# A two-layer graph attention kernel: projections as seven block products, sums through PSUM, two graphs in small steps, spread rows read with a stride

## The chip, the cores and the metric

The kernel runs on one core of a Trainium2 chip. A core has five engines that work side by side, each through its own queue in order: TensorE (PE in the profile; matrix products and transposes, into PSUM), VectorE (DVE), ScalarE (ACT), GpSimd (POOL) and SyncE (SP, which here only issues DMAs). The 128 partitions of the on-chip memory SBUF are the rows of every tile. PSUM has eight banks; one bank holds 512 f32 values per partition. An engine that needs what another makes waits on a semaphore, and so does one that wants to overwrite a buffer that another still reads.

The metric is the time of one execution on the device in microseconds (us). Before the change it is 3888.38 us, the median of three runs (3888.18 to 3889.19).

## The reference

There are 64 graphs of N = 256 nodes with 512 features each, and a 0/1 matrix `adj` of 256 x 256 per graph. Two layers are applied, both with a layer norm ahead and the input added behind. The first layer holds two graph attentions (4 heads of 256, then 1 head of 512), the second one (8 heads of 64). Cut to what matters:

```python
h = maximum(layernorm(x), 0)                      # layer 0
#   gat_layer, once with H=4, F=256 and once with H=1, F=512:
xl = (h @ W).reshape(B, N, H, F)
asrc, adst = einsum('bnhf,hf->bnh', xl, a_src), einsum('bnhf,hf->bnh', xl, a_dst)
e = leaky_relu(asrc[:, :, None, :] + adst[:, None, :, :], 0.2)
attn = softmax(where(mask[..., None], e, -1e9), axis=1)      # over the sources
out = einsum('bsdh,bshf->bdhf', attn, xl) + bias
#   between the two: elu
x = x + out
h = maximum(layernorm(x), 0)                      # layer 1
xp = h @ W_proj                                   # 8 heads of 64
scores = leaky_relu(a_src[:, :, :, None] + a_dst[:, :, None, :] + b_att, 0.2)
att = softmax(where(adj > 0, scores, -1e30), axis=-1)
x = x + relu(att @ xh)
```

So each graph needs three projections: 256 x 512 by 512 x 1024, 256 x 1024 by 1024 x 512, and 256 x 512 by 512 x 512, all in f32.

## The kernel before, in words

A graph's 256 nodes lie as two tiles of 128 (T = 2). `short_path` computes everything without subtracting a maximum in the softmax; at the end it checks that no exponential came too near the limits, and `general_path`, which is not run on this data, would do the work again.

The softmax weight of an edge is exp(leaky_relu(a + b)). The kernel writes it as a product of one-dimensional exponentials: for a source with value a and a target with value b, exp(0.2(a + b)) times the larger of 1 and exp(0.8(a + b)). It therefore needs only exponentials of per-node numbers, some of them spread over all partitions as rows, and one multiply and maximum per edge and head. The extra columns of the weight matrices (N1, N2, N3) make a projection give those per-node numbers (`ex1`, `ex2`, `ex3`) along with the features.

`steps(b)` is a generator with the work of one graph in eight pieces:

- piece 0: load x and adj (SP), build the mask (`mask`, `cap`; DVE, transposes on PE), layer norm, transposed and with relu (`norm_relu_t`, L106 to L128; its `rstd` is a power on GpSimd, L116), and x plus the second bias on GpSimd (L170);
- piece 1: first projection (L184: four blocks of columns, two node tiles, four chunks of 128 features each, so 32 products); ACT takes each result out of PSUM, scaled (L188);
- piece 2: edge weights `e` on DVE (L196), attention products (L204), division and bias (L207, L209), elu (L211 to L213);
- piece 3: transposes of z (L222) with copies on ACT or DVE (L223), second projection (L232: 32 products);
- piece 4: edge weights and products of the second attention (L243, L251), the sum with x (L257), layer norm again;
- piece 5: third projection (L268: 16 products), the exponentials (L271, L272);
- pieces 6 and 7: the eight heads in two groups of four: a weighing on ACT (`wy`, L286), the edge weight on DVE (L287), products with 65 columns (L294), division (L298), the last sum on GpSimd (L303), the store.

The per-node numbers reach all partitions through `over_partitions` (L131): two transposes of a few columns on PE (L135), a copy to SBUF (L137), a DMA of the rows to DRAM (L139) and a DMA that reads them back into every partition (L141). The rows lie whole, one head after the other.

Two graphs are in flight: `order` (L370) interleaves the eight pieces of a graph with those of the one before it. Within this, a scheduling layer places each engine's instructions when the kernel is built, by buffers that come free. Products use five PSUM banks (`ps_mm`), transposes three (`ps_tr`). Before the first graph the attention vectors are folded into the extra columns of the weights (GpSimd products, DVE sums; L337 to L363).

Of the kernel before, what the change touches and what calls it, by code (L numbers as in the profile page):

```python
# [8 lines left out]
F32 = mybir.dt.float32  # L9
BF16 = mybir.dt.bfloat16  # L10
I32 = mybir.dt.int32
# [26 lines left out]
def fold(nc, pool, name, dst, w, a, heads, width):  # L38

    prod = pool.tile([P, heads * width], F32, name=name)  # L40
    pv = prod.rearrange("p (h f) -> p h f", h=heads)
    nc.gpsimd.tensor_tensor(pv, w.rearrange("p (h f) -> p h f", h=heads), a, ALU.mult)
    nc.vector.tensor_reduce(dst, pv, AX.X, ALU.add)
# [3 lines left out]
def short_path(ctx, tc, flags, x, adj, w1, att_src1, att_dst1, b1, w2, att_src2, att_dst2, b2, w_proj, w_att,  # L47
# [13 lines left out]
    assert N == 2 * P and D == D2 == H3 * K3 == 512 and H1 == G and H3 == 2 * G and F1 == D2 // 2  # L61

    const = ctx.enter_context(tc.tile_pool(name="const", bufs=1))
    io = ctx.enter_context(tc.tile_pool(name="io", bufs=3))
# [3 lines left out]
    ps_mm = ctx.enter_context(tc.tile_pool(name="ps_mm", bufs=5, space=PSUM))  # L68
# [21 lines left out]
    N1, N2, N3 = 3 * H1, 3, 3 * H3  # L90
    w1_sb = const.tile([P, DC, HF + N1], F32, name="w1_sb")
    w2_sb = const.tile([P, HC, D2 + N2], F32, name="w2_sb")
    wp_sb = const.tile([P, DC, D + N3], F32, name="wp_sb")
    HALF = D2 // 2
# [3 lines left out]
    wb = const.tile([P, H3], F32, name="wb")  # L98
    xl3s = []
    for i in range(2):  # L100
        xl3 = const.tile([P, T, H3, K3 + 1], F32, name=f"xl3_{i}")
        nc.gpsimd.memset(xl3[:, :, :, K3:], 1.0)
        xl3s.append(xl3)


    def norm_relu_t(src):  # L106
# [14 lines left out]
        hT = work.tile([P, DC, N], F32, name="hT")  # L121
        for c2 in range(DC // 2):
            pt = ps_tr.tile([P, 2, N], F32, name="pt")
            for k in range(2):
                for t in range(T):
                    c = 2 * c2 + k
                    nc.tensor.transpose(pt[:, k, t * P:(t + 1) * P], h[:, t, c * P:(c + 1) * P], ident)  # L127
            nc.scalar.activation(hT[:, 2 * c2:2 * c2 + 2, :], pt, AF.Relu)  # L128
        return hT

    def over_partitions(w, n, bufs):  # L131

        pr = ps_tr.tile([P, 2, N], F32, name="pt")
        for t in range(T):
            nc.tensor.transpose(pr[:n, 0, t * P:(t + 1) * P], w[:, t, :], ident)  # L135
        row = small.tile([n, N], F32, name=f"row{n}", bufs=2)
        nc.vector.tensor_copy(row, pr[:n, 0, :])  # L137
        kept = dram.tile([n, N], F32, name=f"kept{n}")
        nc.sync.dma_start(kept, row)  # L139
        bc = work.tile([P, n, N], F32, name=f"bc{n}", bufs=bufs)  # L140
        nc.sync.dma_start(bc.rearrange("p h n -> p (h n)"), rows_of(kept, n * N))  # L141
        return bc


    def steps(b):
        xs = io.tile([P, T, D], F32, name="xs")
        nc.sync.dma_start(xs, x[b].rearrange("(t p) d -> p t d", p=P))
        ad = io.tile([P, T, N], I32, name="ad", bufs=2)
        nc.sync.dma_start(ad, adj[b].rearrange("(t p) n -> p t n", p=P))


        mask = work.tile([P, T, N], BF16, name="mask")
        nc.vector.scalar_tensor_tensor(mask, ad, 0.0, eye, ALU.is_gt, ALU.max)
        a01 = work.tile([P, T, N], BF16, name="a01")
        nc.vector.tensor_scalar(a01, ad, 0.0, None, ALU.is_gt)
        deg = small.tile([P, T], F32, name="deg")
        nc.vector.tensor_reduce(deg, a01, AX.X, ALU.add)
        none = small.tile([P, T], F32, name="none")
        nc.vector.tensor_scalar(none, deg, 0.5, EVEN, ALU.is_lt, ALU.mult)
        for t in range(T):  # L160
            nc.vector.tensor_scalar(a01[:, t, :], a01[:, t, :], OPEN, none[:, t:t + 1], ALU.mult, ALU.add)
        cap = work.tile([P, T, N], BF16, name="cap", bufs=3)
        pt = ps_tr.tile([P, T, N], BF16, name="pt")
        for t in range(T):
            for s in range(T):
                nc.tensor.transpose(pt[:, t, s * P:(s + 1) * P], a01[:, s, t * P:(t + 1) * P], ident_h)
        nc.any.tensor_copy(cap, pt)

        hT = norm_relu_t(xs)
        nc.gpsimd.tensor_tensor(xs, xs, b2_sb[:, None, :].to_broadcast([P, T, D]), ALU.add)  # L170
        exs = small.tile([P, T * (N1 + N2 + N3)], F32, name="exs")
        ex1 = exs[:, :T * N1].rearrange("p (t n) -> p t n", t=T)
        ex2 = exs[:, T * N1:T * (N1 + N2)].rearrange("p (t n) -> p t n", t=T)
        ex3 = exs[:, T * (N1 + N2):].rearrange("p (t n) -> p t n", t=T)
        yield

        xl = work.tile([P, T, H1, F1 + 1], F32, name="xl1", bufs=1)
        for k in range(H1):
            n = F1 + (N1 if k == 0 else 0)
            at = k * F1 + (N1 if k else 0)  # L180
            for t in range(T):
                pm = ps_mm.tile([P, 512], F32, name="pm")
                for c in range(DC):
                    nc.tensor.matmul(pm[:, :n], hT[:, c, t * P:(t + 1) * P], w1_sb[:, c, at:at + n],  # L184
                                     start=(c == 0), stop=(c == DC - 1))
                if k == 0:
                    nc.scalar.activation(ex1[:, t, :], pm[:, F1:n], AF.Exp)
                nc.scalar.activation(xl[:, t, k, :F1], pm[:, :F1], AF.Copy, scale=ex1[:, t, k:k + 1])  # L188
            if k == 0:
                bc1 = over_partitions(ex1[:, :, 2 * H1:], H1, 1)  # L190
                nc.gpsimd.tensor_copy(xl[:, :, :, F1], ex1[:, :, :H1])
        yield
        e = work.tile([P, T, H1, N], F32, name="e1", bufs=1)
        for h in range(H1):
            for s in range(T):
                nc.vector.scalar_tensor_tensor(e[:, s, h, :], bc1[:, h, :], ex1[:, s, H1 + h:H1 + h + 1],  # L196
                                               mask[:, s, :], ALU.max, ALU.mult)
        z = work.tile([P, T, HF], F32, name="z", bufs=1)
        ez = work.tile([P, T, HF], F32, name="ez", bufs=1)
        for t in range(T):  # L200
            for h in range(H1):
                pm = ps_mm.tile([P, 512], F32, name="pm")
                for s in range(T):
                    nc.tensor.matmul(pm[:, :F1 + 1], e[:, s, h, t * P:(t + 1) * P], xl[:, s, h, :],  # L204
                                     start=(s == 0), stop=(s == T - 1))
                r = small.tile([P, 1], F32, name="r1")
                nc.vector.reciprocal(r, pm[:, F1:F1 + 1])  # L207
                sl = slice(h * F1, (h + 1) * F1)
                nc.vector.scalar_tensor_tensor(z[:, t, sl], pm[:, :F1], r, b1_sb[:, sl], ALU.mult, ALU.add)  # L209

# [443 lines left out]
```

## Time and profile before

| | |
|---|---|
| median of three runs | 3888.38 us |
| the profiled execution | 3889.76 us |
| its span, first to last instruction | 3888.1 us |
| granted TensorE clock, mean | 0.989 |
| busy TensorE, DVE, ACT, GpSimd | 3701.8, 2244.3, 1289.7, 482.6 us |
| first product of the second graph | at 145.12 us |
| first product of the last graph | at 3787.07 us |
| one graph (1202.27 to 1260.99), busy TensorE | 58.72 us, 57.39 us |

How to read what follows. A row of a group names the line in the kernel, the engine, the operation, what it writes and reads, the shape and the count; behind the bars stand the busy time, the mean of one instruction in ns, the idle time of the engine ahead of it and what ended that. A row in order of time has the start, the length, the engine and the same names; in brackets the idle time ahead and what released it. Matmuls overlap one another, so the mean of one (380 ns) is longer than the distance between two starts. An f32 product of a 128 x 128 block shows as two records. Until 145 us the kernel is filling: weights are folded and only one graph runs.

### The profile page before, as it was taken

The numbers are of one execution on the slowest core, as the hardware profiler recorded it, in microseconds if no ns is written. First come the engines' busy times: TensorE is split into PE (matmuls) and PEld (weight loads), VectorE is DVE, ScalarE is ACT, GpSimd is POOL, SyncE is SP. The second block draws the span as 40 slices with busy tenths as digits, with TensorE's granted clock in tenths as the row PEclk, the third lists the DMA queues.
The fourth block names the chain that finished last, engine by engine and source line by source line (L and its number), as shares of the span: only waits on it lengthen the run. The fifth ranks groups of instructions, "written<-read, shape, count | busy, mean of one in ns | idle before, by whom it ended". The sixth has DMA issues, their size and how long they took to land. (4 is left out here: it accounts for less than half of the span.)

```text
span 3888.1 us, 51838 instructions
## 1 busy us (share of the span) xinstructions
PE 3701.8 (95%) x20100; PEld 3213.4 (83%) x20100; DVE 2244.3 (58%) x5780; ACT 1289.7 (33%) x3010; POOL 482.6 (12%) x448
## 2 busy tenths in 40 slices
PE   3799999999999999999999999999999999999998
PEld 2688888888888888888888888888888888888887
DVE  4555655655656556556556556556556556556554
ACT  0223323333333333333333333333333233233332
POOL 5111111111111111101101101101101111111110
PEclk8899999999999999999999999999999999999998
DMA  3011111111111111111111111111111111111111
GB/s 116 28 51 57 49 52 52 54 52 49 57 52 47 59 49 50 59 47 52 54 52 52 48 58 52 49 58 50 51 58 50 51 57 49 52 52 54 50 36 46
DMA packets 86828, 205.34 MB, mean 53 GB/s; under 512 B 7216, under 2 KB 36208, under 8 KB 78384
## 3 DMA queue, kind: packets, MB, share of 16 engines
q1 hardware_dynamic: 81536, 193.82, 14.5%
q10 hardware_dynamic: 4192, 5.24, 0.4%
q8 instruction: 162, 2.65, 0.3%
q0 software_dynamic: 848, 2.89, 0.2%
q14 instruction: 90, 0.74, 0.1%
HBM read 167.51 MB, written 34.41 MB: 52 GB/s over the span
## 5 line engine op out<-in xcount | busy, mean ns | idle before, releaser
L184 PE MATMUL pm<-w_sb,hT 128*128 128x256 f32 (+1 forms) x4096 | 927.9, 384 | 21.9 <-DVE w_sb L331 11.5
L232 PE MATMUL pm<-w_sb,h1T 128*128 128x259 f32 (+1 forms) x4096 | 915.0, 380 | 0.0
L184 PEld LDWEIGHTS pm<-w_sb,hT 128*128 128x128 f32 x4096 | 765.8, 191 | 141.1 <-DVE w_sb L331 13.1
L232 PEld LDWEIGHTS pm<-w_sb,h1T 128*128 128x128 f32 x4096 | 759.3, 189 | 122.2
L287 DVE SCALAR_TENSOR_TENSOR e<-wy,exs,cap 128x256 f32<-128x256 f32 x1024 | 433.3, 482 | 206.4 <-ACT wy L286 206.4
L204 PE MATMUL pm<-xl,e 128*128 128x257 f32 x2048 | 484.4, 384 | 29.4 <-DVE z L209 21.9
L268 PE MATMUL pm<-wp_sb,hT 128*128 128x280 f32 (+1 forms) x2048 | 491.5, 390 | 0.0
L286 ACT ACTIVATE wy<-bc,exs 128x256 f32<-128x256 f32 x1024 | 438.0, 501 | 159.5 <-DMA bc<-kept 155.7
L294 PEld LDWEIGHTS pm<-xl,e 128*128 128x128 f32 x4096 | 478.7, 194 | 7.5 <-DVE e L287 4.2
L294 PE MATMUL pm<-xl,e 128*128 128x65 f32 x4096 | 477.9, 276 | 4.1 <-DVE e L287 4.1
L204 PEld LDWEIGHTS pm<-xl,e 128*128 128x128 f32 x2048 | 381.1, 191 | 84.8 <-issue 32.2
L268 PEld LDWEIGHTS pm<-wp_sb,hT 128*128 128x128 f32 x2048 | 379.6, 190 | 73.1 <-ACT hT L128 0.4
L188 ACT ACTIVATE xl<-pm,exs 128x256 f32<-128x256 f32 x512 | 242.4, 474 | 485.8 <-PE pm L184 477.7
L196 DVE SCALAR_TENSOR_TENSOR e<-bc,exs,mask 128x256 f32<-128x256 f32 x512 | 212.6, 487 | 317.8 <-DMA bc<-kept 288.7
L128 ACT ACTIVATE hT<-pt 128x512 f32<-128x512 f32 x256 | 139.7, 599 | 524.4 <-PE pt L127 524.3
L303 POOL TENSOR_TENSOR o<-o,x 128x1024 f32<-128x1024 f32 x64 | 150.2, 2347 | 987.3 <-DVE o L298 987.3
L116 POOL TENSOR_TENSOR rstd<-ve,neg_half 128x2 f32<-128x2 f32 x128 | 89.0, 695 | 1228.3 <-DVE ve L114 1212.8
L209 DVE SCALAR_TENSOR_TENSOR z<-pm,r,b_sb 128x256 f32<-128x256 f32 x512 | 232.7, 475 | 0.3
L251 PE MATMUL pm<-xl,e 128*128 128x257 f32 (+1 forms) x1024 | 231.9, 379 | 0.0
L137 DVE COPY row<-pt 4x256 f32<-4x256 f32 (+2 forms) x192 | 78.2, 407 | 242.7 <-PE pt L135 242.6
L251 PEld LDWEIGHTS pm<-xl,e 128*128 128x128 f32 x1024 | 193.8, 189 | 27.5
L297 DVE RECIPROCAL r<-pm 128x4 f32<-128x4 f32 x256 | 46.8, 183 | 283.2 <-PE pm L294 283.2
(83 smaller groups left out, 2876.7 us busy)
## 6 DMA issues: line engine op xcount, KB each, us to landing
bc<-kept SPq DMA_DIRECT2D x64, 1024.0 KB
xs<-in_x_dram SPq DMA_DIRECT2D x64, 512.0 KB
bc<-kept SPq DMA_DIRECT2D x64, 512.0 KB
out_dram<-o SPq DMA_DIRECT2D x64, 512.0 KB
ad<-in_adj_dram SPq DMA_DIRECT2D x64, 256.0 KB
bc<-kept SPq DMA_DIRECT2D x64, 128.0 KB
w_sb<-in_L_gnn_W_dram ACTq DMA_DIRECT2D x2, 1024.0 KB
w_sb<-in_L_gnn_W_dram ACTq DMA_DIRECT2D x1, 1536.0 KB
```

Source lines behind the costliest of these rows:

```text
L184: nc.tensor.matmul(pm[:, :n], hT[:, c, t * P:(t + 1) * P], w1_sb[:, c, at:at + n], start=(c == 0), stop=(c == DC - 1))
L188: nc.scalar.activation(xl[:, t, k, :F1], pm[:, :F1], AF.Copy, scale=ex1[:, t, k:k + 1])
L196: nc.vector.scalar_tensor_tensor(e[:, s, h, :], bc1[:, h, :], ex1[:, s, H1 + h:H1 + h + 1], mask[:, s, :], ALU.max, ALU.mult)
L204: nc.tensor.matmul(pm[:, :F1 + 1], e[:, s, h, t * P:(t + 1) * P], xl[:, s, h, :], start=(s == 0), stop=(s == T - 1))
L209: nc.vector.scalar_tensor_tensor(z[:, t, sl], pm[:, :F1], r, b1_sb[:, sl], ALU.mult, ALU.add)
L232: nc.tensor.matmul(pm[:, :n], h1T[:, c, t * P:(t + 1) * P], w2_sb[:, c, at:at + n], start=(c == 0), stop=(c == HC - 1))
L251: nc.tensor.matmul(to[:, :n], e2[:, s, t * P:(t + 1) * P], xl2[:, s, at:at + n], start=(s == 0), stop=(s == T - 1))
L268: nc.tensor.matmul(pm[:, :n], hT[:, c, t * P:(t + 1) * P], wp_sb[:, c, at:at + n], start=(c == 0), stop=(c == DC - 1))
L286: nc.scalar.activation(wy, bc3[:, g + h, :], AF.Copy, scale=ex3[:, s, H3 + g + h:H3 + g + h + 1])
L287: nc.vector.scalar_tensor_tensor(e3[:, s, h, :], wy, ex3[:, s, g + h:g + h + 1], cap[:, s, :], ALU.max, ALU.min)
L294: nc.tensor.matmul(pv[:, h, :], e3[:, s, h, t * P:(t + 1) * P], xl3[:, s, g + h, :], start=(s == 0), stop=(s == T - 1))
L303: nc.gpsimd.tensor_tensor(of, of, x2, ALU.add)
```

## The change

All three projections are done by a scheme with seven block products in place of eight. The matrix product is seen as two by two blocks: rows of nodes (two tiles), the inner dimension in two halves, columns in two halves of 256. With A the left and B the right blocks,

    S1 = A21 + A22   S2 = S1 - A11   S3 = A21 - A11 (signs as in `left`)   S4 = A12 - S2
    T1 = B12 - B11   T2 = B22 - T1   T3 = B12 - B22 (signs as in `right`)  T4 = B21 - T2

seven products of these give the four result blocks as sums. `left` makes the S blocks for every graph and every projection on GpSimd; `right` makes the T blocks once for the weights. The first projection, 1024 columns wide, is two such products (m1a, m1b).

- The sums of products run through PSUM: a bank (`sum`, a new pool of two) goes on being added to while copies of its states are taken to SBUF by ACT (`s1`, `u2`, `u3`); `put` adds such a copy to another bank on DVE, and the last state goes out by ACT.
- The result is no longer scaled on its way out. The extra columns are only 6, 2 and 12 wide; exponentials are taken later from SBUF (`exp1`, `exp2`, `exp3`), for the third attention after adding a bias tile `bl`. Each edge weight is now a weighing on ACT and one operation on DVE in all three attentions (`weigh`); before this held for the third alone.
- The transposes and the row copy of `over_partitions` go. `spread` writes the per-node numbers of all 128 partitions to DRAM as they lie (8 or 2 floats per partition) and reads them back into each partition; the row of a head is then every eighth (second) float of this tile.
- The eight pieces per graph become some fifty small steps, interleaved by a written list. PSUM banks for products fall from five to three, x buffers from three to two, and `xl3` from two to one; edge weights of all attentions share three buffers of 4 KB per partition.
- Turned z goes out by ACT alone, in halves. The sum with x2 goes on GpSimd per quarter and in place; x2 is what is stored.
- Folding of the attention vectors is split over DVE (multiply and sum in one) and GpSimd with ACT; the folds of w2 and wp stand between the steps of the first graph (`weights`).

```diff
+class Product:
...
+    def product(self, to, i, first, last):
+        for c in range(self.nk):
+            self.nc.tensor.matmul(to[:, :self.n], self.lhs[:, i, c, :], self.rhs[:, i, c, :],
+                                  start=(first and c == 0), stop=(last and c == self.nk - 1),
+                                  skip_group_check=True)
+    def kept(self, name):
+        s = self.work.tile([P, 268], F32, name=name)
+        self.nc.scalar.activation(s[:, :self.n], self.sum[:, :self.n], AF.Copy)
+        return s
+    def p1(self):
+        self.sum = self.ps_sum.tile([P, 512], F32, name="sum")
+        self.product(self.sum, 0, True, False)
+        self.s1 = self.kept("s1")
+    def p2(self):
+        pm = self.ps_mm.tile([P, 512], F32, name="pm")
+        self.product(pm, 1, True, True)
+        self.put(0, 0, pm, self.s1)
+    def p5(self):
+        self.pm = self.ps_mm.tile([P, 512], F32, name="pm")
+        self.product(self.pm, 3, True, False)
+    def p6(self):
+        self.product(self.sum, 2, False, False)
+        self.u2 = self.kept("u2")
+    def p7(self):
+        self.product(self.sum, 4, False, False)
+        self.u3 = self.kept("u3")
+    def c22(self):
+        self.put(1, 1, self.pm, self.u3)
+    def p4(self):
+        self.product(self.sum, 5, False, True)
+        self.put(1, 0, self.sum, None)
+    def p3(self):
+        self.product(self.pm, 6, False, True)
+        self.put(0, 1, self.pm, self.u2)
...
-    io = ctx.enter_context(tc.tile_pool(name="io", bufs=3))
+    io = ctx.enter_context(tc.tile_pool(name="io", bufs=2))
-    ps_mm = ctx.enter_context(tc.tile_pool(name="ps_mm", bufs=5, space=PSUM))
+    ps_sum = ctx.enter_context(tc.tile_pool(name="ps_sum", bufs=2, space=PSUM))
+    ps_mm = ctx.enter_context(tc.tile_pool(name="ps_mm", bufs=3, space=PSUM))
...
+    def left(a, nk):
+        a11, a12, s2, s1, s3, a22, s4 = (a[:, i] for i in range(7))
+        nc.gpsimd.tensor_tensor(s1, s3, a22, ALU.add)
+        nc.gpsimd.tensor_tensor(s2, s1, a11, ALU.subtract)
+        nc.gpsimd.tensor_tensor(s3, s3, a11, ALU.subtract)
+        nc.gpsimd.tensor_tensor(s4, a12, s2, ALU.subtract)
+    def relu_left(h):
+        a = work.tile([P, 7, DC // 2, P], F32, name="hs")
+        for r, (upper, lower) in enumerate(((0, 4), (1, 5))):
             pt = ps_tr.tile([P, 2, N], F32, name="pt")
+            turn(lambda t, c: h[:, t, c * P:(c + 1) * P], 2 * r, pt)
+            nc.scalar.activation(a[:, upper], pt[:, :, :P], AF.Relu)
+            nc.scalar.activation(a[:, lower], pt[:, :, P:], AF.Relu)
+        left(a, DC // 2)
+        return a
+    def spread(w, n):
+        kept = dram.tile([P, n], F32, name=f"kept{n}")
+        nc.sync.dma_start(kept, w)
+        bc = work.tile([P, P * n], F32, name=f"bc{n}")
+        nc.sync.dma_start(bc, rows_of(kept, P * n))
+        return bc
+    def total(dst, pm, add):
+        if add is None:
+            nc.scalar.activation(dst, pm, AF.Copy)
+        else:
+            nc.vector.tensor_tensor(dst, pm, add, ALU.add)
...
+    def weigh(dst, bc, xw, yw, mask, op):
+        wy = work.tile([P, T, P], F32, name="wy", bufs=4)
+        nc.scalar.activation(wy, bc, AF.Copy, scale=yw)
+        nc.vector.scalar_tensor_tensor(dst, wy.rearrange("p t q -> p (t q)"), xw, mask, ALU.max, op)
...
+        def exp1(self):
+            nc.scalar.activation(self.ex1.rearrange("p (a j) t -> p a j t", a=2),
+                                 xl1[:, :, 0:2, :L1].rearrange("p t a j -> p a j t"), AF.Exp)
+            self.bc1 = spread(self.exs[:, 16:24], 8).rearrange("p (q h t) -> p h t q", h=H1, t=T)
...
+        def turn2(self, r, k):
+            if r == 0 and k == 0:
+                self.a2 = work.tile([P, 7, HC // 2, P], F32, name="h1s", bufs=1)
+                self.m2 = Product(nc, ps_sum, ps_mm, work, self.a2, w2_sb, put2)
+            pt = ps_tr.tile([P, 2, N], F32, name="pt")
+            turn(lambda t, c: self.zt[t][:, c * P:(c + 1) * P], 4 * r + 2 * k, pt)
+            for i, at in (((0, 0), (4, P)), ((1, 0), (5, P)))[r]:
+                nc.scalar.activation(self.a2[:, i, 2 * k:2 * k + 2], pt[:, :, at:at + P], AF.Copy)
+            if r == 1 and k == 1:
+                left(self.a2, HC // 2)
...
+        def exp3(self):
+            nc.vector.tensor_tensor(lg3, lg3, bl[:, None, :, :].to_broadcast([P, T, 2, L3]), ALU.add)
+            for t in range(T):
+                nc.scalar.activation(self.ex3[:, :, :, t, :].rearrange("p i a h -> p a i h"),
+                                     lg3[:, t].rearrange("p a (i h) -> p a i h", h=G), AF.Exp)
+            self.bc3 = [spread(self.exs[:, 64 + 8 * a:72 + 8 * a], 8).rearrange("p (q t h) -> p h t q", h=G, t=T)
+                        for a in range(2)]
...
+            o = work.tile([P, G, K3], F32, name="o", bufs=4)
+            nc.vector.scalar_tensor_tensor(o, pv[:, :, :K3], 0.0, r.to_broadcast([P, G, K3]), ALU.max, ALU.mult)
+            to = self.x2[:, t, a * Q:(a + 1) * Q]
+            nc.gpsimd.tensor_tensor(to, to, o.rearrange("p h k -> p (h k)"), ALU.add)
...
+    order = """
+        0 m1a p1, 0 m1a p2, 0 m1a p5, 0 m1a p6, -1 edges2, 0 m1b p1, 0 m1a p7, 0 m1a c22, 0 m1b p2, 0 m1a p4,
+        0 m1b p6, 0 m1a p3, 0 exp1, 0 m1b p5, 0 m1b p7, 0 m1b c22, -1 gat2 0, 0 m1b p4, 0 m1b p3, 0 edges1 0,
+        -1 gat2 1, 1 load, -1 norm3, 0 gat1 0 0, 0 edges1 1, 0 gat1 0 1, 0 gat1 1 0, 0 gat1 1 1,
+        -1 turn3, -1 m3 p1, -1 m3 p2, -1 m3 p5, -1 m3 p6, 0 turn2 0 0, 0 turn2 1 0, -1 m3 p7, -1 m3 c22,
+        0 turn2 0 1, 0 turn2 1 1, -1 m3 p4, 0 m2 p1, -1 m3 p3, -1 exp3, 0 m2 p2, 0 m2 p6, 1 masks, 0 m2 p5, 0 m2 p7,
+        0 m2 c22, -1 edges3 0 0, -1 edges3 0 1, -1 gat3 0 0, 0 m2 p4, 1 norm1, -1 gat3 0 1, 0 m2 p3, 0 exp2,
+        -1 edges3 1 0, -1 edges3 1 1, -1 gat3 1 0, 1 turn1, -1 gat3 1 1, -1 store
+    """
```

In the list, 0 is the current graph, -1 the one before it, 1 the next. As in the kernel before, the scheduling layer still places instructions on each engine when it is built, so neighbouring steps overlap. In the compiled order of TensorE, for example, the first of the two products of m3 p6 stands ahead of the last three pairs of gat1's products, and the transposes of the next graph's norm stand between gat3's products.

## The prediction

> **What bounds the kernel now.** I read the page's first lines, then TensorE in order of time over one graph, then the groups of instructions by shape, then the other engines in order of time.
>
> ```profile
> span 3888.1 us, 51838 instructions
> PE 3701.8 (95%) x20100; PEld 3213.4 (83%) x20100; DVE 2244.3 (58%) x5780; ACT 1289.7 (33%) x3010; POOL 482.6 (12%) x448
> ```
>
> TensorE is busy for 95% of the span, the next engine for 58%. In order of time (start, length, what):
>
> ```profile
> 1202.27 3.83 PE L184 MATMUL pm<-w_sb,hT 128*128 128x268 f32 x16
> 1206.59 10.09 PE L184 MATMUL pm<-w_sb,hT 128*128 128x256 f32 x46
> ...
> 1228.33 3.94 PE L268 MATMUL pm<-wp_sb,hT 128*128 128x280 f32 x16
> 1233.28 0.28 PE L135 MATMUL pt<-ident,exs 128*8 128x128 f32 x1 [1.01 <-DVE exs L272]
> ...
> 1238.73 7.16 PE L232 MATMUL pm<-w_sb,h1T 128*128 128x259 f32 x32
> ...
> 1260.99 1.35 PE L184 MATMUL pm<-w_sb,hT 128*128 128x268 f32 x5
> ```
>
> The period of a graph is 1260.99 - 1202.27 = 58.72 us. Only 1.33 us of it is idle TensorE: the 1.01 shown and 0.32 before a transpose at 1223.93. Each f32 product is two records. A record of 256 columns takes (10.09 - 0.17)/46 = 0.2157 us (0.17 is the drain of the last), one of 280 (3.94 - 0.17)/16 = 0.2356: 0.83 ns per column.
>
> Durations used below (group; instances | busy, mean ns):
>
> ```profile
> L286 ACT ACTIVATE wy<-bc,exs 128x256 f32<-128x256 f32 x1024 | 438.0, 501 | 159.5 <-DMA bc<-kept 155.7 <-DVE e L287 3.8
> L287 DVE SCALAR_TENSOR_TENSOR e<-wy,exs,cap 128x256 f32<-128x256 f32 x1024 | 433.3, 482 | 206.4 <-ACT wy L286 206.4
> L209 DVE SCALAR_TENSOR_TENSOR z<-pm,r,b_sb 128x256 f32<-128x256 f32 x512 | 232.7, 475 | 0.3
> L273 ACT COPY xl<-pm 128x256 f32<-128x256 f32 x256 | 95.3, 372 | 237.0 <-PE pm L268 233.0
> L360 POOL TENSOR_TENSOR z<-wp_sb,ez 128x256 f32<-128x256 f32 x16 | 11.2, 722 | 6.9 <-DVE va L363 5.6 <-DVE va L351 1.3
> ```
>
> The trip of spread numbers through DRAM, and a DVE operation that a GpSimd one held up:
>
> ```profile
> 1206.79 0.41 DVE L137 COPY row<-pt 4x256 f32<-4x256 f32 x1 [3.68 <-PE pt L135]
> 1207.23 0.27 SPq L139 DMA_DIRECT2D kept<-row  x1
> 1208.50 0.33 SPq L141 DMA_DIRECT2D bc<-kept  x1
> 1211.95 3.25 DVE L196 SCALAR_TENSOR_TENSOR e<-bc,exs,mask 128x256 f32<-128x256 f32 x8 [4.74 <-DMA bc<-kept]
> ...
> 1230.84 2.36 POOL L170 TENSOR_TENSOR xs<-xs,b_sb 128x1024 f32<-128x1024 f32 x1 [3.38 <-DVE h L119]
> 1231.46 1.76 DVE L272 TENSOR_TENSOR exs<-exs,wb 128x8 f32<-128x8 f32 x1
> ```
>
> Write 1.27 us, read back and start 3.45 us. L272 takes 0.15 us alone; here it ends as the GpSimd addition does. L209, with one operand in PSUM, ran unhindered beside the same addition (0.87 us for two).
>
> **TensorE's own sum.** Removed: 80 products per graph (32 of L184, 32 of L232, 16 of L268). At their widths their records cost 13.96 + 13.88 + 7.22 = 35.06 us. Added: 14 products of 262 columns (28 x 0.2207 = 6.18), 14 of 256 (6.04), 28 of 258 (12.17), 14 of 268 (6.32): 30.71. The six L135 transposes go, 0.11 us each by start to start: 0.66. TensorE's work falls from 58.72 - 1.33 = 57.39 to 52.38 us.
>
> **The other engines per graph.** *ACT* (20.1 us busy now): 26 weighings at 0.50 (16 now) 13.0; 12 partial sums and 4 last sums out of PSUM at 0.38: 6.1; 8 relu and 8 turn copies at 0.38: 6.1; exponentials and mask about 4. Sum 29. *DVE* (34.5 now): 12 additions from PSUM, not seen before; ends 0.40 (the L137 copy) and 0.48 (L209), I take 0.45, near L209 because it too reads PSUM and SBUF. That adds 5.4 and three small ones 0.5; the rows, h1T copies and L272 go (1.2 + 1.4 + 1.9). About 36. *GpSimd* (6.7 now): four sums before each left operand, 8 x 0.73 and 4 x 1.24 = 10.8, four additions to x2 at 0.75 (the 2.35 of L303 goes), the 2.35 of L170, two rstd: 17.6. None reaches 52, so waits decide.
>
> **Waits, with engines in program order.** I laid the compiled order over one period with these durations (DVE and ACT follow-ups start every 0.40, as L287 x8 in 3.33 shows; 0.2 us from a product's last record to its reader).
> - *Handovers of the running sum*: a copy to SBUF must end before the next product adds: 0.2 + 0.38. One other product (0.86) lies between in m1 and m2; in m3 it is transposes. Cost 0; if an ACT weighing stands in front, 0.4 each.
> - *exp1 to gat1*: addition 0.65 after m1a's last product, exponential 0.2, write 1.27, read back 3.45, weighing 0.50 and DVE 0.48: 6.55. TensorE has 2 + 2 + 4 + 2 + 2 + 4 = 16 products x 0.43 = 6.9 for it. The write is now 128 rows of 32 bytes. Ends: 1.10 us (the one-row write) and 2.9 (the trip of the 128 KB read on 128 partitions); I take 1.6, near the writes. The DVE also waits for gat2's reciprocal first. Stall 0.5.
> - *Three PSUM buffers instead of five for gat1*: its third pair waits until z of the first is written, behind four weighings (1.6) and a bn_stats (0.6); the next likewise: 0.55 + 0.25.
> - *norm3*: bn, rstd on GpSimd 0.70, two h of 0.55, then transposes: 0.6.
> - *m3 p6* stands before gat1's last three products and needs the second GpSimd sum: 0.2 + about 1.2 of relu copies + 2 x 0.75 = 2.9 after the transposes, against 1.2 us of product p1 and a transpose: 1.65.
> - *m2 p6* needs the second wide sum, behind xs + b2: 2.35 + 2.48 after h's second half, 0.45 more than the products there.
> - *exp3 to gat3*: bias add, two exponentials, two writes, 1.27 + 3.45, against 16 products of m2 p2, p6, p5, p7 (6.9) and six transposes: covered, 0.75 left over. If the trip is 1 us longer, 0.25 shows.
> - *SP*: x moves behind gat2's last read of its buffer (two buffers, not three): issued about 17 us into the period, needed at 24; covered by 3 us. The store stands before the next mask load and waits for the x2 addition about 2 us into the period; the spread trip of exp1 begins at 8.8. Covered.
> Sum 4.0 of waits. A restart after each of the six costs 0.1: 0.6. The old 1.33 goes with its causes (L272 gone; the 0.32 is in norm3's 0.6).
>
> **Two unknown prices.** *Collisions*: 17.6 us of GpSimd sums beside about 17 us of DVE operations with both inputs in SBUF. If none meet, 0; if met at random, 17.6/57.8 x 17 = 5.2. I take 0.5, near 0, because most GpSimd sums fall where DVE waits for TensorE; the one that matters is the bias add before exp3, up to 1.24 with 0.75 of slack. *The strided read*: no row reads SBUF with a step. It can't gain, for the count of elements stays. Other end: each element twice; ACT pays (599 - 372)/256 = 0.89 ns per element (L128 against L273), so 0.23 per weighing, 24 x 0.23 = 5.5. In the order above half of that is slack of ACT; I take 0.3 on the path, near the contiguous L286.
> [...]
>
> Period 52.4 + 4.0 + 0.6 + 0.8 = 57.8 us.
>
> **Ends.** Before: the second graph's first product starts at 145.12, the last graph's at 3787.07 (62 periods of 58.74), and 101.0 follow. After: half the folds of w1 and w2 move from GpSimd to DVE, and the block sums are added. GpSimd up to the second graph: 48 folds x 0.73, 10 of block sums, 16 of the rest: 61, from about 10 on, with 10 of waits; then gat1, transposes and m2, 30: 110. Ends: 97 (no waits) and 145 (no gain). The last graph: a period (57.8) from its first product to its gat2, then alone what takes 44.5 now (first L251 of the last graph at 3843.62 to the span's end); the relu and block sums added there (about 3) I set against the shorter last addition to x2 and the earlier store: 102. Sum 110 + 62 x 57.8 + 102 = 3796. The profiled execution is 3889.76 and its span 3888.1; the median of the runs is 3888.38, 0.3 above the span, which I let go.
>
> **Rivals.**
> - *The trip after exp3 decides (slower).* Place: the bias add to gat3's first product. Price: strided weighings 16 x 0.23 = 3.7 and a write of 2.9 instead of 1.6 make 5.0, less the slack of 0.75: 4.2, period 62, 212 + 62 x 62 = 4056. It decides from 1.5 us of it: 212 + 62 x 59.3 = 3888. For it: the in-order ACT has two partial-sum copies between the weighings. Against: 16 weighings overlap gat3 and m2.
> - *GpSimd against DVE (slower).* All 5.2 in place of 0.5: 62.5, 4087; half of it, 60, 3932. For it: L272. Against: the places.
> - *The waits overlap more than I lay out.* A third of the 4.6: 54.7, 3603. For it: one stall shifts what follows it. Against: m3 p6 has nothing in front.
> - *No gain at all:* waits take just what the products give, 59.3: 3888.
>
> **How the numbers follow.** Forecast (3700 to 3880) 0.52; overlap 0.14; exp3 trip 0.16; collisions 0.13; no gain 0.05. Runs of this kernel differ by 0.03%, so 0.2% is about what can be told from no change. Faster 0.52 + 0.14 + a little of the collisions: 0.67; same 0.03; slower 0.30. Two in ten are left out by 3610 and 3990; the forecast's own range is 3700 to 3880.
>
> **What would show it.** Period about 57.8 with TensorE busy 52 to 53; the longest idle before m3's third product, released by GpSimd; weighings still near 500 ns; bias add under 0.3; write trip under 2. Wrong: weighings of 700, DVE operations stretched to GpSimd's ends, or idle before gat3 of over 2 us; a clock below 1.00 in the middle (after 3.09 us idle at 3850.39 eight transposes took 2.00 instead of 1.04).

## The result, and the profile after

The changed kernel takes 4095.1 us, the median of four runs (4080.69 to 4097.53), against 3888.78 us (four runs, 3888.18 to 3890.57): 1.052 times as long (95% interval 1.0497 to 1.0547). It is slower where I forecast 3796 us. The profiled execution is the one of 4080.69 us, with a mean granted clock of 0.980 (the other three: 0.976), so the sums below are made against its span of 4079.0.

The first lines of the page after:

```profile
span 4079.0 us, 52874 instructions
...
PE 3618.3 (89%) x18436; PEld 2950.0 (72%) x18436; DVE 2469.6 (61%) x6660; ACT 1996.8 (49%) x4417; POOL 1206.3 (30%) x1284
```

TensorE is busy for 83.5 us less than before and idle for 4079.0 - 3618.3 = 460.7 us instead of 186.3. No engine has taken its place as the bound. The names of the steps stand in `order` above; p1 to p7 are the seven block products of a projection. One graph of TensorE in order of time (start, length, what; in brackets the idle time ahead and what ended it), cut to the waits:

```profile
1951.34 0.41 PE L387 MATMUL pm<-xl,e 128*128 128x65 f32 x2
...
1954.79 2.67 PE L387 MATMUL pm<-xl,e 128*128 128x65 f32 x22 [0.20 <-DVE e L238]
...
1966.61 1.02 PE L54 MATMUL sum<-w1b_sb,hs 128*128 128x256 f32 x4
1970.10 2.08 PE L54 MATMUL sum<-w1a_sb,hs 128*128 128x262 f32 x4 [2.46 <-ACT u L60]
1971.97 1.70 PE L54 MATMUL pm<-w1b_sb,hs 128*128 128x256 f32 x4
1973.51 1.05 PE L54 MATMUL sum<-w1a_sb,hs 128*128 128x262 f32 x4
...
1983.76 3.51 PE L305 MATMUL pm<-xl,e 128*128 128x257 f32 x12 [0.54 <-DVE e L238]
1987.64 2.09 PE L305 MATMUL pm<-xl,e 128*128 128x257 f32 x8 [0.37 <-DVE r L308]
...
1993.49 0.72 PE L54 MATMUL sum<-wp_sb,hs 128*128 128x268 f32 x2 [1.16 <-POOL hs L188]
...
2007.71 2.01 PE L54 MATMUL sum<-w_sb,h1s 128*128 128x258 f32 x8 [0.15 <-POOL h1s L188]
...
2013.70 0.33 PE L387 MATMUL pm<-xl,e 128*128 128x65 f32 x2
```

This period is 2013.70 - 1951.34 = 62.36 us (62 periods: 62.08 on average; forecast 57.8). Its longest wait is none of those I had listed. Product p7 of m1a waits 2.46 us for `u2`, a copy on ACT, and the eight records behind it take 1.87 + 1.54 us where others of their widths take 0.88 + 0.87: 1.66 more. ACT and SP at that place:

```profile
1961.45 0.20 ACT L331 ACTIVATE exs<-xl 128x8 f32<-128x8 f32 x1
...
1964.16 0.39 ACT L60 ACTIVATE s<-sum 128x262 f32<-128x262 f32 x1 [1.49 <-PE sum L54]
1968.74 0.93 ACT L237 ACTIVATE wy<-bc,exs 128x256 f32<-128x256 f32 x2 [4.20 <-DMA bc<-kept]
1969.58 0.37 ACT L60 ACTIVATE u<-sum 128x262 f32<-128x262 f32 x1
```

```profile
1961.67 0.32 SPq L206 DMA_DIRECT2D kept<-exs  x1
1964.48 0.32 SPq L208 DMA_DIRECT2D bc<-kept  x1
```

`u2` is a copy of 0.37 us whose input, the bank after p6, was ready at about 1966.8; p7 adds to the same bank, so it can't start before the copy has ended. Ahead of it in ACT's order stand the two weighings of the second attention (`edges2`, of the graph before), and these wait for `exp2`'s numbers to come back from DRAM: exponential at 1961.45, write at 1961.67, read at 1964.48, data at 1968.7. The write alone takes 2.81 us here. The page's DMA part (KB each, us from issue to landing) sets it apart from the other writes:

```profile
kept<-exs SPq DMA_DIRECT2D x192, 4.0 KB, 1.4
...
kept<-exs SPq DMA_DIRECT2D x64, 1.0 KB, 3.1
```

From all partitions 8 floats each land in 1.4 us, 2 floats each in 3.1. The read lands 4.2 us after its issue at the median, where the trip of the same 128 KB had taken 2.9 before the change; why it is slower was not followed. The stretched records are a clock that falls. First this place, then one of the graphs that don't pay (after the times: the stretch's length, busy time and instructions of PE, PEld, DVE, ACT, POOL, then the granted clock and DMA):

```profile
1966.49:1969.90 3.41, 1.15 (x6) 0.66 (x4) 0.93 (x4) 1.16 (x4) 0.05 (x1) 1.00 0.77 192
1969.90:1973.32 3.42, 3.22 (x8) 2.59 (x9) 1.42 (x3) 0.71 (x3) 0.00 (x0) 0.50 0.28 78
1973.32:1976.73 3.41, 3.41 (x17) 2.97 (x16) 0.81 (x2) 0.77 (x2) 0.00 (x0) 1.00 0.01 3
```

```profile
1843.61:1847.02 3.41, 1.86 (x9) 1.28 (x7) 1.01 (x3) 0.00 (x0) 0.77 (x2) 1.00 0.67 129
1847.02:1850.43 3.41, 1.95 (x9) 1.75 (x10) 1.95 (x4) 1.87 (x5) 0.00 (x0) 1.00 0.18 66
1850.43:1853.84 3.41, 3.41 (x18) 2.95 (x17) 0.92 (x3) 0.95 (x3) 0.00 (x0) 1.00 0.28 74
```

After the 2.46 us of idleness the granted clock is 0.50 for 3.4 us. Not every graph pays this: at 1785.75 the same product is stretched to 2.08 us after 2.87 us of idleness, at 1848.48, 1909.35 and 2032.73 it takes 1.12 after 3.01, 2.65 and 2.82. The length of the idleness doesn't decide it, its place does. In this trace all 59 changes of the granted clock lie on one grid of 3.41 us, and the stretches above are stretches of that grid. The idleness of 2.46 us lies in one stretch but for 0.2 us, which leaves TensorE busy for 1.15 of 3.41 us; the one of 3.01 us is cut in two by the grid. From 103 to 4035 us, 25 of the 26 falls follow a stretch in which TensorE was busy for 12 to 40% (the other: 54%), and none follows the 1097 others at full clock, in which it was busy for 41% or more. That is no threshold, even here: one fall follows 54%, and 22 of the 1097 were busy for 41 to 54%.

The groups that answer to the prices:

```profile
L237 ACT ACTIVATE wy<-bc,exs 128x256 f32<-128x256 f32 x1664 | 1102.2, 734 | 551.8 <-DMA bc<-kept 545.3
L238 DVE SCALAR_TENSOR_TENSOR e<-wy,exs,cap 128x256 f32<-128x256 f32 x1024 | 499.3, 493 | 480.6 <-ACT wy L237 461.9
...
L215 DVE TENSOR_TENSOR xl<-pm,u 128x256 f32<-128x256 f32 (+2 forms) x512 | 216.6, 423 | 354.2 <-ACT u L60 181.3
```

A weighing takes 734 ns on average against 501 before (the 24 per graph with a step of eight floats 750 at the median, the two with a step of two 515); an addition from PSUM 423 (taken: 450). Over the whole run TensorE's waits are (us in total, times, longest):

```profile
PE sum L54 <- ACT u L60: 181.6, 66, 3.6
PE sum L54 <- POOL hs L188: 73.1, 63, 1.2
PE pm L305 <- DVE e L238: 34.7, 67, 2.2
```

### The profile page after: what moved, and what is told of

Same layout as the page of the kernel before. It is cut to its first block, busy times and chain, and to the rows that moved or that the text cites. A ratio compares the mean times of both kernels' runs of the same rounds, so it can differ in the third digit from the quotient of the medians.

```text
span 4079.0 us, 52874 instructions
## 1 busy us (share of the span) xinstructions
PE 3618.3 (89%) x18436; PEld 2950.0 (72%) x18436; DVE 2469.6 (61%) x6660; ACT 1996.8 (49%) x4417; POOL 1206.3 (30%) x1284
## 4 chain that ended last, share of the span: by engine, by line
issue 41%; ACT 20%; POOL 14%; DMA 9%; PE 9%; DVE 6%; ACTq 0%; POOLq 0%; SPq 0%
ACT wy L237 15%; DMA bc<-kept 7%; PE sum L54 4%; POOL rstd L172 3%; DMA kept<-exs 3%; DVE h L175 2%; POOL hs L190 2%; PE pt L182 2%; POOL hs L187 2%; POOL hs L188 2%; POOL x L394 2%; POOL hs L189 2%; ACT hs L198 2%; PE pm L54 2%; ACT hs L199 2%
## 5 line engine op out<-in xcount | busy, mean ns | idle before, releaser
L237 ACT ACTIVATE wy<-bc,exs 128x256 f32<-128x256 f32 x1664 | 1102.2, 734 | 551.8 <-DMA bc<-kept 545.3
L305 PE MATMUL pm<-xl,e 128*128 128x257 f32 x2048 | 536.5, 399 | 60.0 <-DVE e L238 34.7
L387 PE MATMUL pm<-xl,e 128*128 128x65 f32 x4096 | 548.2, 273 | 33.0 <-DVE e L238 31.7
L54 PE MATMUL sum<-w_sb,h1s 128*128 128x258 f32 x2048 | 544.6, 393 | 13.7 <-POOL h1s L188 12.8
L54 PE MATMUL sum<-w1a_sb,hs 128*128 128x262 f32 x1024 | 316.2, 424 | 199.8 <-ACT u L60 180.0
L238 DVE SCALAR_TENSOR_TENSOR e<-wy,exs,mask 128x256 f32<-128x256 f32 x640 | 304.3, 484 | 230.5 <-ACT wy L237 228.1
L215 DVE TENSOR_TENSOR xl<-pm,u 128x256 f32<-128x256 f32 (+2 forms) x512 | 216.6, 423 | 354.2 <-ACT u L60 181.3
L54 PEld LDWEIGHTS sum<-w_sb,h1s 128*128 128x128 f32 x2048 | 364.7, 190 | 83.9 <-POOL h1s L188 38.2
L54 PE MATMUL sum<-wp_sb,hs 128*128 128x268 f32 x1024 | 314.4, 409 | 80.6 <-POOL hs L188 73.1
L54 PE MATMUL pm<-w_sb,h1s 128*128 128x258 f32 x1536 | 370.5, 383 | 0.0
L54 PEld LDWEIGHTS pm<-w_sb,h1s 128*128 128x128 f32 x1536 | 287.4, 190 | 41.5
L54 PE MATMUL sum<-w1b_sb,hs 128*128 128x256 f32 x1024 | 265.2, 382 | 0.5 <-ACT u L60 0.5
```

The source lines that it names most:

```text
L54: self.nc.tensor.matmul(to[:, :self.n], self.lhs[:, i, c, :], self.rhs[:, i, c, :], start=(first and c == 0), stop=(last and c == self.nk ...
L215: nc.vector.tensor_tensor(dst, pm, add, ALU.add)
L237: nc.scalar.activation(wy, bc, AF.Copy, scale=yw)
L238: nc.vector.scalar_tensor_tensor(dst, wy.rearrange("p t q -> p (t q)"), xw, mask, ALU.max, op)
L305: nc.tensor.matmul(pm[:, :Q + 1], e[:, k, s, t * P:(t + 1) * P], xl1[:, s, h, L1:], start=(s == 0), stop=(s == T - 1))
L387: nc.tensor.matmul(pv[:, h, :], self.e3[2 * a + h // 2][:, h % 2, s, t * P:(t + 1) * P], xl3[:, s, a * G + h, :], start=(s == 0), stop=(s ...
```

## The experiments

My theory from this profile: the trip of `exp2` is late, `u2` stands behind its weighings, and the clock falls in the wait; the step in the reads adds to it. Rival 1: weighings with a step and the trip after `exp3` set the period wherever a wait is taken away. Rival 2: GpSimd's sums slow the DVE. The queues' orders come from the scheduling layer, not from the written list alone. Orders are therefore set by an edge (`issue_after`) that lets an instruction issue only behind another on its engine.

### edges2 moved behind u3, whole rows, and both

```diff
 def edges2(self):
-    for s in range(T):
-        weigh(...)
+    with tc.issue_after(graphs[self.b + 1].m1[0].last):    # u3 of m1a
+        for s in range(T):
+            weigh(...)
```

> One place in ACT's order is changed: the two weighings of the second attention (edges2) stand behind u3 of the next graph's m1a instead of ahead of u2. My theory: the second attention's spread numbers land 4.2 us after the read is issued and ACT stands still for them, with u2 behind it; so TensorE's 2.46 us before m1a's product p7 go, and with them the 1.67 us by which the next eight products were stretched. Period 62.36 - 4.13 = 58.2 us, total 3820 to 3845. Rival 1 (the strided weighings and the trip after exp3 set the period): the wait only moves, 4060 to 4095. Rival 2 (GpSimd sums slow the DVE): no change, 4080 to 4095.

```diff
-spread(self.exs[:, 16:24], 8).rearrange("p (q h t) -> p h t q", h=H1, t=T)
+spread(self.exs[:, 16:24], 8).rearrange("p (h t q) -> p h t q", h=H1, t=T)
 ... (the other two spreads likewise)
```

> The tile that was read back is read as if each row lay whole (128x256 without a step); DMAs, counts and order stay as they are. The weights are then those of other nodes, so the output is not the reference's; the time is that of reads without a step. Weighings should fall from 0.73 to 0.50 us. My theory: exp2 stands behind weighings on ACT and starts 1.4 us earlier, so the 2.46 us before m1a's p7 fall to about 1.0, and the stretch after it goes or stays: period 59.3 to 61.0, total 3890 to 4010. Rival 1 (the strided weighings decide): back to 57.8 or 58, 3800 to 3840. Rival 2 (collisions): 4060 to 4095.

> Both edits at once (again with weights of other nodes, so not the reference's output). My theory: the price of the step that is left once edges2 is moved is small, 0.25 before gat1 and 0.2 before gat3: 0.3 to 0.6 us a graph, 3785 to 3820. Rival 1: the same as with whole rows alone. Rival 2: 4050 to 4090.

| | median us | ratio to before, 95% | us per graph |
|---|---|---|---|
| changed kernel | 4095.1 | 1.0497 to 1.0547 | 62.08 |
| edges2 moved | 3876.8 | 0.9956 to 0.9979 | 58.83 |
| whole rows | 3831.3 | 0.9828 to 0.9861 | 58.16 |
| both | 3747.9 | 0.9621 to 0.9653 | 56.82 |

The graphs' average is taken from the third graph's first product to the last graph's, 61 periods. "Whole rows" reads numbers of other nodes in both of its runs.

Moving two weighings gives 218 us: rival 1, by which the wait only moves, falls, and rival 2 as the main cause too (GpSimd's order is unchanged; the DVE's changed only in that two edge weights follow their weighings). It is 32 to 57 us short of what I expected: gat1 now waits 63.0 us in all for its edge weights instead of 34.7, and the wait at `u2` with its low clock had cost about 3.6 us a graph on average (worked out at the end), not the 4.13 of the graph that I had looked at. TensorE's waits with `edges2` moved:

```profile
PE sum L54 <- POOL hs L188: 73.0, 63, 1.2
PE pm L305 <- DVE e L238: 63.0, 67, 2.3
PE pm L388 <- DVE e L238: 31.7, 88, 6.5
```

The row of `u` is gone. The step costs more than my theory held: whole rows alone came out in rival 1's range (3800 to 3840), not in mine, and both edits lie below all the ranges. With `edges2` moved, whole rows save 58.83 - 56.82 = 2.01 us a graph where I expected 0.3 to 0.6, and without the move 3.92, since `exp2` then no longer stands behind a queue of late weighings: it starts 0.03 us after its addition instead of 1.7, and the wait for `u2` falls from 181.6 us in all to this:

```profile
PE sum L54 <- ACT u L60: 76.9, 66, 3.2
```

The orders of all five engines are the same with whole rows alone as in the changed kernel. So the late weighings and the step are not two separate prices: the step makes `exp2` late, and `exp2` makes `u2` late. Either edit alone brings the time back into the forecast range of 3700 to 3880. Which reads pay shows in the changed kernel by shape, first a stretch with weighings of the third attention, then the two of the second:

```profile
L237 ACT ACTIVATE wy<-bc,exs 128x256 f32<-128x256 f32 x6 | 4.1, 760 | 0.0
```

```profile
L237 ACT ACTIVATE wy<-bc,exs 128x256 f32<-128x256 f32 x2 | 0.9, 514 | 4.2 <-DMA bc<-kept 4.2
```

With a step of eight floats 760 ns, of two floats 514; with whole rows 496 at the median. Why the wider step costs so much more is not shown.

### The write of exp2, alone

```diff
-self.bc2 = spread(self.exs[:, 28:30], 2).rearrange("p (q t) -> p t q", t=T)
+self.bc2 = spread(self.exs[:, 24:32], 8, "bc2", 1).rearrange("p (q i t) -> p i t q", i=4, t=T)[:, 2]
```

The last of these runs has this edit, and edges on the order that leave all five engines' orders as in the changed kernel from the second graph on; the first has only an edge that keeps `edges2` ahead of `u2`. Both also give the two weighings of `edges2` a step of eight floats.

> The changed kernel with edges2 where it was, ahead of u2 on ACT, but exp2 writes 8 floats of each partition instead of 2 (and reads 512 KB back instead of 128). My theory: the write of 8 bytes per partition takes 3.11 us, of 32 bytes 1.44; the data land 1.67 earlier, the two weighings are 0.25 longer each, and TensorE's wait of 2.9 us a graph before m1a's p7 falls to about 1.5; with part of the stretch after it: 4095 to 3980 or 4030. Rival (the arrival of these numbers isn't what u2 waits for): 4080 to 4100.

> The changed kernel with the 32-byte write and 512 KB read for exp2 as before, and with m1a's p7 held ahead of m1b's p2, so that the order on all five engines is that of the changed kernel and only this one transfer differs. (Without that hold p7 had moved behind m1b's p2, and m3's p6 behind three pairs of gat1: 57.63 us a graph.) My theory: the numbers land 1.67 earlier and the two weighings ahead of u2 take 0.25 longer each, so the wait before p7 falls by 1.2 from 2.9 us on average to about 1.7, the stretch after it from about 1.7 to 0.8 or nothing: 59.2 to 60.1 a graph, 3910 to 3970. If it were only the order that made the difference there: 4060 or more. If only the write: 3780 to 3820.

With nothing but the transfer (and that step) changed: 3909.7 us (ratio to before 1.004 to 1.0074), 185 less than the changed kernel, 59.40 us a graph, at the lower end of what I expected. SP and TensorE at that place, and TensorE's waits:

```profile
2003.16 0.32 SPq L206 DMA_DIRECT2D kept<-exs  x1
2004.57 0.32 SPq L208 DMA_DIRECT2D bc<-kept  x1
```

```profile
2010.22 1.12 PE L54 MATMUL sum<-w1a_sb,hs 128*128 128x262 f32 x4 [1.10 <-ACT u L60]
2011.18 1.02 PE L54 MATMUL pm<-w1b_sb,hs 128*128 128x256 f32 x4
```

```profile
PE sum L54 <- POOL hs L188: 73.1, 63, 1.2
PE sum L54 <- ACT u L60: 63.6, 66, 1.8
```

The write takes 1.41 us, and the read of four times the bytes lands sooner than the small one (3.6 us against 4.2 at the median). From the start of `exp2` to the first weighing it is 5.37 us instead of 7.67 (medians): of the 2.30, the write gives 1.7 and the read 0.6, and 0.47 go back in the two longer weighings. The wait for `u2` falls by 118.0 us, 1.87 a graph, and TensorE is busy for 3571.5 us instead of 3618.3: 46.8 less, about what the mean granted clock says (0.991 instead of 0.980 of 4079 us: 45). Together 164.8 of the 173.0 us between the two spans. After 1.10 us of idleness the next eight records (0.96 and 0.86) are hardly stretched.

The first run came out below all that I had expected of it (3980 to 4030). Where the layer could choose, it put m1a's p7 behind m1b's p2 and m3's p6 behind the next three pairs of gat1: 3793.8 us, ratio 0.9736 to 0.9769, 57.63 us a graph. Of the wait for `u2` 3.3 us in all are left, of those of 1.16 for GpSimd's sum none; gat1 waits 65.8 in all and transposes for their `h` 53.2 (23.9 with the transfer alone changed, 20.8 of it once at the start). This version leaves nothing out of the computation and beats both kernels. How its 116 us divide between p7 and p6 was not taken apart.

### The order of a load, and what it upset

In the kernel with `edges2` moved, the write of `exp1` had slowed from 1.44 to 1.86 us (medians), with adj's load of the next graph 0.7 to 1.5 us ahead of it.

```diff
+first = nc.sync.dma_start(self.xs, ...).ins
-nc.sync.dma_start(self.ad, ...)
+with tc.issue_after(first):
+    nc.sync.dma_start(self.ad, ...)
```

> As with edges2 moved, and the load of the next graph's adj is issued behind the load of its x, so behind the spread trip of exp1, instead of about 1.2 us ahead of it. With edges2 moved the write of exp1 took 1.86 us from issue to the read's issue (median; 10 of 61 over 2.3, the longest 3.38), where it had taken 1.44 with the adj load 4.58 us or more ahead. My theory: the two transfers meet, and gat1 waits for it (63 us in all on the first weights): writes back to 1.44, period 58.83 to 58.1, total 3815 to 3850. Rival (the write's time scatters by itself): within 0.3% of 3877.

> The same, and the tile that was read back is read as if its rows lay whole (weights of other nodes, not the reference's output). It gives the price of the step that is left when nothing else is late. My theory: 56.82 to about 56.4 a graph, 3710 to 3735, so the step costs 1.6 us a graph. Rival (with the trips out of the way ACT has room, as the prediction held): at most 0.5 us a graph below the kernel with only adj and edges2 moved.

Right about the write (1.44 again, at most 2.17), wrong about the time: 3994.6 us (1.0247 to 1.0282), 118 slower. With whole rows it is 3853.6 where I expected 3710 to 3735, but the step's price holds up (60.77 - 58.59 = 2.18 a graph). The longest wait is now gat3's, 151.2 us in all. With adj loaded at another time the layer had ordered the DVE anew (and some steps of ACT and GpSimd); the DVE's rows, and GpSimd's:

```profile
1966.33 2.89 DVE L175 TENSOR_SCALAR h<-xs,mv,rstd 128x512 f32<-128x512 f32 x2 [0.82 <-POOL rstd L172]
1969.14 0.16 DVE L215 TENSOR_TENSOR lg<-pm,u 128x12 f32<-128x12 f32 x1
1969.22 0.41 DVE L215 TENSOR_TENSOR xl<-pm,u 128x256 f32<-128x256 f32 x1
1969.55 0.86 DVE L368 TENSOR_TENSOR lg<-lg,bl 128x48 f32<-128x48 f32 x1
```

```profile
1966.27 1.26 POOL L187 TENSOR_TENSOR h1s<-h1s 128x512 f32<-128x512 f32 x1
1967.61 1.33 POOL L188 TENSOR_TENSOR h1s<-h1s 128x512 f32<-128x512 f32 x1
1968.90 1.45 POOL L189 TENSOR_TENSOR h1s<-h1s 128x512 f32<-128x512 f32 x1
```

The next graph's two `h` stand ahead of the bias add of `exp3`, end one by one, each 0.28 us behind a wide sum of GpSimd, and take 1486 ns each at the median instead of 539. The bias add takes 0.86 instead of 0.20, and gat3, whose trip had 0.75 us to spare in my working, waits 2.16 us. So rival 2 is real as a mechanism, but not in the changed kernel, where `h` never took more than 550 ns. An edge that keeps `h` behind the bias add:

> As the kernel with edges2 and adj moved (3994.6 us), and on the DVE the two h of the next graph's norm1 are issued behind the bias add of exp3. There they had stood ahead of it, beside GpSimd's wide sums, and took 2.89 us instead of 1.1, so that exp3 and its trip were late and TensorE waited 2.16 us before gat3 (151 us in all). My theory: that wait goes, and the clock's drop after it: 60.77 to 58.0 or 58.3 a graph, 3815 to 3850, a little below the kernel with edges2 alone moved (3877). Rival (the adj load behind x harms in itself, by meeting another transfer): 3940 or more.

3848.7 us (0.9884 to 0.9917): at the upper end of what I expected, and 28 us below the kernel with `edges2` moved. `h` still takes 1489 ns beside GpSimd's sums, but the bias add no longer stands behind it; that takes 0.60 us, and gat3 still waits 74.8 us in all (31.7 with `edges2` alone moved). So the order made most of the harm, and some is left. Two runs put m3's p6 behind gat1's last three pairs, the first without that repair, the second with it:

> As the kernel with edges2 and adj moved, and m3's product p6 is issued behind gat1's last three pairs of products instead of ahead of them. My theory: the 1.16 us that TensorE waits there for the second GpSimd sum (73 us in all) are filled by those products: 1.1 us a graph less, 3745 to 3785. Rival (the wait moves on to z and the products behind it): less than 0.4 us a graph.

> The same with m3's p6 behind gat1's last three pairs. Without the repair of the DVE's order this gained 0.14 us a graph, since m3's p2 then waited 0.72 for a PSUM buffer (45 us in all) where p6 had waited 1.16. My theory: 0.4 us a graph below the kernel without this edit, 3785 to 3825. Rival (p6's wait costs nothing, because something later decides): the same within 0.2%.

3989.0 and 3841.2 us: 0.14 and 0.12 us a graph less (60.63 and 58.27; the times of the single runs overlap for the first pair, not for the second). Both of my numbers were too low, and both rivals hold. The wait for GpSimd's sum (74 us) goes, and 45 us of it come back as p2 waiting for a PSUM buffer that gat1 frees; most of the rest is in TensorE's busy time, 13 and 16 us longer, and why was not followed.

### The old way to spread

```diff
-bc = spread(...)    # strided rows
+bc = over_partitions(...)    # transposes, row copy, whole rows, as before the change
```

> The same, but the spread is done as before the change: transposes of the per-node numbers on TensorE, a row copy on the DVE, a write of whole rows, weighings without a step. TensorE gets 8 transposes more (0.9 us a graph), the DVE 4 copies (1.6), the trip of exp1 about 0.9 more. If the step costs 1.6 us a graph, the two ways come out about even: 58.0 to 58.6 a graph, 3820 to 3865. If the step is nearly free, this is slower by 1 to 2 us a graph: 3880 to 3960.

> The same with the spread as before the change (8 transposes on TensorE, 4 row copies on the DVE, whole rows). With the repaired order the step should still cost about 2 us a graph (whole rows gained 58.83 - 56.82 = 2.0 and 60.77 - 58.59 = 2.2), and the old way 0.9 of TensorE and up to 0.9 of the trip of exp1: 0 to 1 us a graph faster, 3730 to 3825. Rival: the transposes wait in TensorE's queue for the exponentials and the old way is slower by 1 us or more, over 3860.

4015.7 and 4022.5 us (1.0315 to 1.0349 and 1.0318 to 1.0363), the first above both of its ranges: weighings of 494 ns and a write of 1.10 us for `exp2`, and yet 61.1 and 61.3 us a graph. The second is over 3860, as its rival had it, but the transposes' wait for the exponentials is only a part of that: 32.8 us in all (123.8 in the first run). In the second run gat3 waits 90.1 us (74.7 without the old way), gat1 63.4 (31.7), transposes for `h` 54.5 (24.8), m3's p2 48.2 (45.2), sums for `u` 32.0 (2.0), and TensorE is busy for 87 us more, the new transposes included, at a mean clock of 0.974 instead of 0.990. Taking the step away this way costs more in queues than the 2 us it brings. So the 2 us of whole rows are a bound and not yet a version; another way to have them was not tried.

## Why the prediction was wrong, point by point

- *What bounds the kernel, and TensorE's sum.* TensorE stayed the engine that all wait for, and its removed and added products came out near. In the period above its work is 57.26 us against 52.38. Of the 4.88 more, 1.95 are m1a's and m1b's records, mostly at the low clock, about 1.1 gat1's records, which come at the pace of the weighings, and 0.57 the transposes of `h` (booked as a wait of 0.6). Some 1.4 are a real miss: m2's products cost 12.80 instead of 12.17, m3's 6.82 instead of 6.32, z's transposes 2.06 instead of 1.77 before, and the run with both edits shows the same three.
- *Handovers of the running sum: "Cost 0; if an ACT weighing stands in front, 0.4 each."* **This is the step that failed.** Two weighings did stand in front of `u2`, and their price was not 0.4 but the wait for their data: 2.46 us and 1.66 of low clock here, 2.88 and about 0.7 on average (181.6/63 and 46.8/63). Moving them gave 218 us, a quicker trip of that data 185. The term that made this wait long was mis-sized too: the strided read, two points below.
- *The write of the spread.* 1.6 us taken for 32 bytes per partition: 1.44. But `exp2` writes 8 bytes per partition, and its trip is missing from the list of waits altogether. At 3.1 us its write lies outside both of my ends (1.10 and 2.9), its read takes 4.2 us where I had 2.9 for such a read in hand, and `exp2` itself starts 1.7 us after its addition, behind weighings.
- *The strided read.* The end "each element twice", my estimate, gave the right price (750 ns against 501 with a step of eight floats: 0.25 more, forecast 0.23), but not for every step (515 with two floats); "half of that is slack of ACT; I take 0.3 on the path" was not: 2.0 us a graph with the trip out of the way, 3.9 with it, where the sum had 0.3. ACT has slack on average and none in front of gat1 and `exp2`, where the weighings stand in a row.
- *The other waits.* gat1 0.54 (0.5), PSUM buffers 0.37 (0.8), m3's p6 1.16 (1.65), m2's p6 0.15 (0.45), gat3 0.20 (covered, up to 0.25), the transposes of z 0.22 (not listed). A restart cost 0.08 (0.96 against 0.88 for the four records after a wait; the 0.1 taken was a guess that no run shows). Without the 4.12 us at `u2` this period would be 58.24 against 57.8. That closeness is partly luck: too little work and too long waits cancel.
- *Collisions.* 0.5 taken; the bias add is 0.197 at the median, `h` unhindered. Right here for those two, though one order away from 2 us. (`ez` and `a01` are stretched once a graph, to 0.87 and 0.83 us at most; what that costs was not followed.)
- *SP.* Right for x and the store. *Ends.* The second graph's first product is at 110.08 (110). From the last graph's first product, at 3958.82, to the end it is 120.2 us (102): the same wait of 2.83 us occurs there, and over the last 129 us the granted clock is 0.83.
- *The rivals.* "Weighings of 700" came, but not where the first rival put them: gat3 waits 0.20. Its period of 62 us is the measured one by luck: the wait stood before m1a's p7. Two of the signs that I gave for a wrong forecast were seen, weighings of 700 and a clock below 1.00 in the middle. In sum: (62.08 - 57.8) x 62 = 265 us and 18 of the end make 3796 into 4079; the other three runs are 12 to 17 us longer, at the clock of 0.976.

## What to carry to other kernels

For every transfer that brings an engine its input, ask what else stands behind that input in the engine's order, and cost the trip for its own shape, the small ones first (a write of 8 bytes per partition took 3.1 us here, of 32 bytes 1.4). A wait on the pacing engine can cost more than its length, where the clock falls with it (here 2.46 us of wait and 1.66 of stretched records). A change of one issue time can reorder other queues, so after each edit read the order of all engines before reading the time.

## What the runs showed of the hardware that was not expected

- A DMA write of 8 bytes from each of 128 partitions to DRAM took 3.1 us (median), of 32 bytes 1.4; reading back the 128 KB took 4.2 us (2.9 before the change, where one row of 1 KB had been written) and 512 KB 3.6 to 4.0.
- An f32 read by ScalarE with a step of two floats took 514 ns for 256 elements, with eight floats 760, without a step 496.
- The granted clock fell to 0.50 for 3.4 us after idle stretches of 2.46 and 2.87 us of TensorE, and not after 2.65, 2.82 and 3.01. It changed only on a grid of 3.41 us, and in the changed kernel 25 of 26 falls followed a stretch of the grid that was busy for at most 40%: what counted here is how much of the idleness fell into one stretch.
- DVE operations with one SBUF input of 512 f32 per partition took 1486 ns beside GpSimd's additions instead of 539 (adj's load moved). The two shown there ended 0.28 us behind one of these each; why is not shown.
